# Issuing the second row gather of each pair beside the first, and normalizing three ticks earlier in even steps

## The chip, the cores and the metric

The kernel runs on one core of one Trainium2 chip. The metric is the device time of one launch in microseconds (us), given as the median of several runs. A profile of one execution gives a span, from the first to the last instruction of the program, and what each engine did in it: TensorE (PE), VectorE (DVE), ScalarE (ACT), GpSimd (POOL) and the queue that issues plain DMAs (SP).

## What is computed

A batch of 16 graphs with 1024 nodes and 128 features goes through two layers, each with a residual.

```python
h = relu(layernorm(x)); x = x + attention(h, adj)      # layer 0: softmax over neighbours
h = relu(layernorm(x)); x = x + sage3(h, adj, nodemask) # layer 1
# sage3 starts with this, on each graph's 1024x1024 adjacency:
def step(carry, n):                 # n = 0..1023, each row depends on the rows before it
    row = carry[n]; num = row.sum()
    sf = (num + 1) // 2 if num > 10 else 1
    rm = row & (cumsum(row) % sf == 0) & (num > 1)
    carry[n] = row & ~rm; carry[:, n] &= ~rm
# then three rounds of (adj_d @ h) / deg, two matmuls with weights, l2 norm, relu, batch norm,
# and one last matmul on the three results side by side
```

The sequential pass over rows is called dilation here. A row with 2 to 10 neighbours left at its turn loses them all, so the kernel finds by a bound the rows that may have more (at most 128 per graph), gathers only those rows of the adjacency from memory, and solves the rule for them by a fixed number of iterations.

## The kernel before

**Stages.** The first stage runs 16 steps, one per graph. A step computes scores and values of attention for its graph, and beside them, in pieces, the preparation of later work. From 770 us on a second stage does the first round of layer 1 (function `mix`), together with the rest of the dilation of the last four graphs. Two more rounds and the output follow.

**Ticks.** A step has 48 ticks. Its body is a loop over 16 score tiles (`scores`, L704: two hardware matmuls each); a tick follows the score matmul, and each of the two groups of value matmuls (`values`, L720) that come after it. So there is one score tile in three ticks, and its number times three is the tick. At every tick a hand-written agenda advances generators: each generator is a function cut by `yield` into parts, and a list gives the tick of each part. Parts are emitted in the order of the agenda within a tick, and each engine executes what is emitted for it in this order. What reads a result of another engine is often put off by one or more ticks (`later`).

**Beside attention, in step i:** `bound` of graph i (L237 to L244: a few very small matmuls, L240 and L241, then a comparison into `d_away`, L243, eight times in turn), `mirrors` (transposes L193 and their comparison L199), `project` of graph i+1 (normalization, then projections), loading the adjacency of graph i+1 (ACT, L167 and L184), `norms_of_x2` and `store` of graph i-1, and the solver `solve` for groups of four graphs, which is active in steps 5 to 7 and 9 to 15. `project` on POOL has a chain of small operations (`moments`, L583 to L589) and eight normalizations (`normalize`, L595); PE transposes their results (L605). `norms_of_x2` has the same chain of small operations. `store` issues eight indirect DMAs (L547) on POOL.

**Pairs and gathers.** In every odd step the nodes of two graphs are sorted together (`sort`), and then `gather` is planned for both, in 13 parts: four parts build one-hot tiles on DVE (L298, two instructions each); a fifth multiplies them on PE to node numbers (L303); a sixth turns these into row numbers on DVE (L306) and issues the indirect DMA on POOL (L308) that brings up to 128 rows, 512 KB, into the tile `rows`; the seventh scans the rows on DVE (L312), the eighth makes `codes` of them (L315); the ninth transposes these on PE (L319) into a PSUM tile; two parts copy this on ACT (L323); the twelfth multiplies with the one-hots (L327); the thirteenth stores the codes that the solver needs (L330 to L334). `AT_GATHER` (L750) has the ticks of both, counted from the odd step's start: from 48 on they lie in the next, even step. The tiles `rows`, `left`, `codes` and `turned` have one buffer each.

**PSUM.** The results of `bound`, `mirrors`, `sort` and `gather` go to tiles called `pd`, which take turns in two buffers, in the order in which they are emitted. A new tile in a buffer waits until the readers of the tile before in that buffer are done.

**The last pair.** After step 15 the agenda runs 22 ticks more. What then remains of the last gather is advanced evenly over the 120 turns of the second stage (`last_of_dilation`, L915), with empty turns after some parts (`GATHER_IDLE`), and the solver for the last four graphs follows.

Of the kernel before, what the change touches and what calls it, by code (L numbers as in the profile page):

```python
# [9 lines left out]
H16 = mybir.dt.float16  # L10
# [5 lines left out]
P = 128  # L16
B, N, D = 16, 1024, 128
NB = N // P
# [13 lines left out]
S = 2 * P  # L32
# [48 lines left out]
class Dilation:  # L81
# [209 lines left out]
    def gather(self, b):  # L291


        nc = self.nc
        used = self.used[:, b:b + 1]
        onehot = self.pool.tile([P, NB, S], H16, name="onehot", bufs=1)
        for k in range(NB):
            nc.vector.tensor_scalar(onehot[:, k, :], self.iota, self.pick[b - b % 2][:, b % 2, k:k + 1], None, op0=OP.is_equal)  # L298
            if k % 2:
                yield  # L300
        pi = self.bank([P, 1], F32)
        for k in range(NB):
            nc.tensor.matmul(pi, onehot[:, k, :P], self.node16[:, k:k + 1], start=(k == 0), stop=(k == NB - 1))  # L303
        yield
        row = self.pool.tile([P, 1], I32, name="row")
        nc.vector.tensor_scalar(row, pi, float(b * N), None, op0=OP.add)  # L306
        rows = self.pool.tile([P, N], F32, name="rows", bufs=1)
        nc.gpsimd.indirect_dma_start(out=rows, out_offset=None, in_=self.adj.rearrange("b n m -> (b n) m"),  # L308
                                     in_offset=bass.IndirectOffsetOnAxis(ap=row[:, 0:1], axis=0))
        yield  # L310
        left = self.pool.tile([P, N], H16, name="left", bufs=1)
        nc.vector.tensor_tensor_scan(left[:, ::-1], rows[:, ::-1], rows[:, ::-1], 0.0, op0=OP.add, op1=OP.bypass)  # L312
        yield
        codes = self.pool.tile([P, N], H16, name="codes", bufs=1)
        nc.vector.scalar_tensor_tensor(codes, rows, 1023.0, left, op0=OP.mult, op1=OP.add)  # L315
        yield
        pt = self.bank([P, NB, P], H16)
        for k in range(NB):
            nc.tensor.transpose(pt[:, k, :], codes[:, k * P:(k + 1) * P], self.identh)  # L319
        yield  # L320
        turned = self.pool.tile([P, NB, P], H16, name="turned", bufs=1)
        for h in range(2):
            nc.scalar.activation(turned[:, 4 * h:4 * h + 4, :], pt[:, 4 * h:4 * h + 4, :], AF.Copy)  # L323
            yield
        pq = self.bank([P, S], F32)
        for k in range(NB):
            nc.tensor.matmul(pq, turned[:, k, :], onehot[:, k, :], start=(k == 0), stop=(k == NB - 1))  # L327
        yield
        dg = self.pool.tile([P, P], BF, name="dg")
        nc.vector.scalar_tensor_tensor(dg, pq[:, :P], used, self.identf, op0=OP.mult, op1=OP.mult,  # L330
                                       accum_out=self.dcode[:, b:b + 1])
        nc.vector.tensor_scalar(self.own[:, b, :], dg, 512.0, None, op0=OP.is_gt)
        nc.vector.scalar_tensor_tensor(self.code[:, b, :P], pq[:, :P], used, self.up, op0=OP.mult, op1=OP.mult)
        nc.scalar.activation(self.code[:, b, P:], pq[:, P:], AF.Copy, scale=used)  # L334
        yield
# [172 lines left out]
@with_exitstack  # L508
def gnn_kernel(ctx: ExitStack, tc: tile.TileContext, a, out):
    nc = tc.nc  # L510
    with tc.tile_pool(name="verdict", bufs=1) as vp:
        flag = fast(tc, a, out, vp)
        bad = nc.values_load(flag[0:1, 0:1])
    tc.strict_bb_all_engine_barrier()
    with tc.If(bad > 0):
        general(tc, a, out)
# [3 lines left out]
def fast(ctx: ExitStack, tc: tile.TileContext, a, out, vp):  # L520
# [127 lines left out]
    with ExitStack() as s1:  # L648
# [83 lines left out]
        def store(b):  # L732
            for k in range(NB):
# [7 lines left out]
        every = lambda first, n, by: [first + by * j for j in range(n)]  # L741

        AT_PROJECT = [m + every(m[4] + 4, 4, 1) + every(m[4] + 12, 10, 3)
                      for m in ([1, 9, 14, 15, 16], [0, 1, 3, 5, 6])]
        AT_LOAD = every(1, 2 * NB, 3)
        AT_BOUND = [[0] + [first + 3 * (j // 2) + j % 2 for j in range(2 * NB)] for first in (9, 3)]
        AT_MIRRORS = ([11, 20, 23, 29, 33, 35, 39, 42, 44], [11, 13, 16, 19, 22, 25, 29, 33, 41])

        AT_SORT = [27, 29, 31, 32, 33, 35, 36]
        AT_GATHER = ([37, 38, 39, 41, 44, 45, 51, 55, 59, 60, 61, 65, 66],  # L750
                     [68, 69, 70, 71, 74, 75, 81, 85, 89, 90, 91, 93, 94])
        AT_NORMS = ([30, 57, 67, 68, 71], [42, 44, 58, 67, 70])
        AT_STORE = every(75, NB, 2)

# [4 lines left out]
        def plan(gen, start, ticks):  # L759
            agenda.append((gen, [start + t for t in ticks]))  # L760

        def solve_pieces(b0, b1):
            return 9 * ITER + 3 + 13 * (b1 - b0)

        def plan_step(i):
# [13 lines left out]
            if odd:  # L779
                plan(dil.sort(i - 1), start, AT_SORT)  # L780
                for b, ticks in zip((i - 1, i), AT_GATHER):
                    gathering[b] = dil.gather(b)
# [127 lines left out]
    load_x2(2)  # L910


    GATHER_IDLE = {5: 6, 7: 5}

    def last_of_dilation():  # L915

        for part in range(13 - gather_left, 13):
            next(gathering[B - 1])
            for _ in range(1 + GATHER_IDLE.get(part, 0)):
                yield  # L920
# [161 lines left out]
    with tc.tile_pool(name="ps1", bufs=2, space=PSUM, reuse_waits="tile") as ps:  # L1082
# [5 lines left out]

        tick, TICKS1, PIECES1 = 0, 8 * (B - 1), gather_left + sum(GATHER_IDLE.values()) + solve_pieces(LAST, B)
        entering = iter(())  # L1090
# [786 lines left out]
```

## Time and profile before

| | us |
|---|---|
| time, median of 3 runs | 1275.23 (1273.57 to 1277.38) |
| span of the profiled execution | 1230.9 |
| time of the profiled execution as a whole | not given beside the profile |
| PE busy | 1106.3 |
| DVE busy | 883.8 |
| ACT busy | 728.2 |
| POOL busy | 567.2 |

A line of groups has the line, engine, operation, result and inputs with their shapes and the number of instructions; then the busy time, the mean of one in ns, and after the second bar the idle time of the engine just before them with what ended most of it. A line of the timeline has the start in us from the span's start, the length, the engine, the line, the operation, the number of instructions merged, and in brackets the idle time before. The end of a matmul is modelled, so a busy PE is not PE at its peak; starts are measured. A line of busy time by windows has the window, its length, then the busy time and number of instructions of PE, PE's weight loads, DVE, ACT and POOL, then PE's granted clock, the share of the DMA engines and GB/s.

### The profile page before, as it was taken

Reading aid. Unit: us, or ns where it says so; the run is one execution under the profiler, and the core shown is the slowest. Engines: PE = TensorE matmul, PEld = TensorE weight load, DVE = VectorE, ACT = ScalarE, POOL = GpSimd, SP = SyncE. Lnnn points to the kernel's source line nnn. Section 1 sums busy time; section 2 is a strip of 40 time slices with the busy share of each in tenths; the row PEclk is TensorE's granted clock in tenths of the full one; section 3 lists DMA queues with packets and bytes.
Section 4 is the critical chain, followed back from the end, with each engine's and each line's share of the span. In section 5 each row is a group of like instructions: output and inputs, shape, how many; then the busy total and the mean of one; then the engine's idle time right before and its main releaser. Section 6 shows DMA issues by size and latency. Waiting matters only on the chain.

```text
span 1230.9 us, 22315 instructions
## 1 busy us (share of the span) xinstructions
PE 1106.3 (90%) x7787; PEld 824.2 (67%) x7787; DVE 883.8 (72%) x2630; ACT 728.2 (59%) x1570; POOL 567.2 (46%) x1043
## 2 busy tenths in 40 slices
PE   7899999999899899899889888778769979999896
PEld 3566676666576576567567656667657868888775
DVE  6767567579778678778777868688887876666632
ACT  5578788677678678678677752346554543333221
POOL 0330752651743643644535434687410003777775
PEclk8899999999899999999999999889999999999998
DMA  6544244344234344344333410334000012877664
GB/s 209 148 135 138 87 140 153 106 124 150 87 120 152 103 125 155 95 129 139 109 114 106 130 59 27 96 101 115 1 1 1 1 32 78 237 232 214 195 184 134
DMA packets 118146, 143.44 MB, mean 117 GB/s; under 512 B 9212, under 2 KB 94088, under 8 KB 118024
## 3 DMA queue, kind: packets, MB, share of 16 engines
q1 hardware_dynamic: 106120, 110.78, 30.1%
q0 software_dynamic: 11904, 31.15, 7.7%
q8 instruction: 63, 1.03, 0.4%
q14 instruction: 59, 0.48, 0.1%
HBM read 113.39 MB, written 28.51 MB: 115 GB/s over the span
## 4 chain that ended last, share of the span: by engine, by line
PE 56%; DVE 23%; ACT 6%; POOL 6%; issue 4%; DMA 4%; POOLq 0%; DVEq 0%; ACTq 0%; SPq 0%
PE ps L704 10%; PE po L720 10%; PE po L970 6%; PE pm L683 6%; DVE e L707 4%; DMA rows<-in_adj_dram,row 4%; PE pt L1026 3%; PE ph L1194 2%; PE ph L1251 2%; DVE left L312 2%; PE ph L1195 2%; POOL hn L595 2%; PE po L975 2%; ACT e L706 2%; DVE m L369 2%
## 5 line engine op out<-in xcount | busy, mean ns | idle before, releaser
L720 PEld LDWEIGHTS po<-vw,e 128*128 128x128 f32 x2048 | 274.0, 195 | 66.5 <-issue 66.1
L720 PE MATMUL po<-vw,e 128*128 128x129 f32 x2048 | 307.8, 285 | 0.0
L704 PE MATMUL ps<-qT,kT 128*128 128x512 f32 x512 | 273.3, 617 | 0.8 <-ACT e L706 0.8
L707 DVE TENSOR_TENSOR e<-e,ab 128x512 f32<-128x512 f32 x256 | 177.6, 695 | 113.0 <-ACT e L706 111.3
L706 ACT ACTIVATE e<-ps 128x512 f32<-128x512 f32 x256 | 153.0, 598 | 108.2 <-PE ps L704 85.4
L547 POOL DMA_INDIRECT x_d<-xt,slot x128 | 143.6, 1122 | 39.8 <-issue 36.1
L167 ACT ACTIVATE ab<-st,d_one_k 128x1024 bf16<-128x1024 f32 x128 | 146.8, 1147 | 0.0
L583 POOL TENSOR_SCALAR ln_t<-ln_st 128x8 f32<-128x8 f32 x31 | 8.0, 260 | 290.3 <-DVE ln_st L576 233.2
L184 ACT ACTIVATE junk<-st 128x1024 bf16<-128x1024 f32 x112 | 118.2, 1056 | 0.0
L547 POOL DMA_INDIRECT y_d<-y,nodes x88 | 86.5, 983 | 28.9 <-issue 28.3
L729 ACT ACTIVATE o<-po,recips 128x128 f32<-128x128 f32 x128 | 46.8, 368 | 72.4 <-DVE recips L727 72.2
L704 PEld LDWEIGHTS ps<-qT,kT 128*128 128x128 f32 x512 | 79.1, 194 | 8.2 <-issue 3.7
L595 POOL TENSOR_SCALAR hn<-xt,ln 128x128 f32<-128x128 f32 x120 | 76.4, 648 | 1.6
L1038 ACT ACTIVATE r<-pt 128x512 f32<-128x512 f32 x74 | 44.4, 601 | 55.3 <-PE pt L1026 55.3
L984 ACT ACTIVATE sq<-po 128x512 f32<-128x512 f32 x80 | 47.7, 596 | 48.0 <-PE po L975 44.0
L970 PE MATMUL po<-ws,r 128*128 128x128 f32 x512 | 72.8, 286 | 0.0
L1035 DVE BATCH_NORM_STATS2 stats<-r 128x6 f32<-128x512 f32 x74 | 50.8, 687 | 29.2 <-ACT r L1038 29.2
L987 DVE TENSOR_REDUCE nrm<-sq 128x4 f32<-128x512 f32 x80 | 53.9, 676 | 24.6 <-ACT sq L984 23.3
L312 DVE TENSOR_TENSOR_SCAN left<-rows 128x1024 f16<-128x1024 f32 x16 | 38.9, 2432 | 45.1 <-DMA rows<-in_adj_dram,row 45.1
L1169 POOL COPY mark<-y 128x1 f32<-128x1 f32 x30 | 5.8, 192 | 137.1 <-DVE y L1043 134.5
L970 PEld LDWEIGHTS po<-ws,r 128*128 128x128 f32 x512 | 63.0, 194 | 8.6 <-issue 6.8
L199 DVE SCALAR_TENSOR_TENSOR junkv<-pd,ab 128x64 bf16<-128x64 int32 (+7 forms) x128 | 57.8, 451 | 15.1 <-PE pd L193 15.1
(303 smaller groups left out, 2433.2 us busy)
## 6 DMA issues: line engine op xcount, KB each, us to landing
st<-in_adj_dram SPq DMA_DIRECT2D x128, 512.0 KB, 3.7
r<-y_d SPq DMA_DIRECT2D x22, 512.0 KB, 6.5
xt<-x_d SPq DMA_DIRECT2D x16, 524.0 KB, 4.0
xt<-in_x_dram SPq DMA_DIRECT2D x16, 512.0 KB, 4.3
x<-x_d SPq DMA_DIRECT2D x16, 512.0 KB, 4.6
out_dram<-r SPq DMA_DIRECT2D x11, 512.0 KB, 3.3
x_d<-xt,slot POOLq DMA_INDIRECT x128, 2.8
y_d<-y,nodes POOLq DMA_INDIRECT x88, 5.4
```

Source lines behind the costliest of these rows:

```text
L167: nc.scalar.activation(ab[:, k, :], st, AF.Exp, bias=self.one_k, scale=ONE_K, accum_out=self.deg[:, b, k:k + 1])
L184: nc.scalar.activation(junk(), st, AF.Exp, scale=-ZERO_K, accum_out=zeros)
L199: nc.vector.scalar_tensor_tensor(junk.rearrange("p a b -> p (a b)")[:, :n], pt.rearrange("p a b -> p (a b)").bitcast(I32)[:, :n], 1.0, ab[ ...
L312: nc.vector.tensor_tensor_scan(left[:, ::-1], rows[:, ::-1], rows[:, ::-1], 0.0, op0=OP.add, op1=OP.bypass)
L547: d = nc.gpsimd.indirect_dma_start(out=dst, out_offset=bass.IndirectOffsetOnAxis(ap=slots, axis=0), in_=src, in_offset=None)
L595: engine.tensor_scalar(hn[:, k, :], xt[:, k, :D], minus[:, k // 2, k % 2, None], rstd[:, k // 2, k % 2, None], op0=OP.add, op1=OP.mult)
L683: nc.tensor.matmul(pp, w, hT[:, 512 * g:512 * g + 512], start=True, stop=True)
L704: nc.tensor.matmul(p, K[b][:, k * P:(k + 1) * P], Q[b][:, c], start=True, stop=True)
L706: later(1, lambda: nc.scalar.activation(e, p, AF.Exp))
L707: later(2, lambda: nc.vector.tensor_mul(e, e, AB_[b][:, k, c]))
L720: nc.tensor.matmul(po[:, q % 2, :], E[k][:, i * P:(i + 1) * P], V[b][:, k, :], start=(k == 0), stop=(k == NB - 1))
L970: nc.tensor.matmul(po[:, i, :], hT[:, c:c + P], wxk, start=(i == 3), stop=False)
```

## The change

Four edits. The second gather of each pair has its first six parts (one-hots, node numbers, row numbers and DMA) at ticks 48 to 61 instead of 68 to 75; its scan stays at tick 81 and all later parts where they were. The first gather of each pair has these six parts at ticks 37 to 41 instead of 37 to 45; its scan stays at 51. The one-hot tile gets a second buffer, since the second gather's one-hots are now written before the first gather has read its own for the last time (tick 65). In even steps the normalization for the next graph is planned 2 to 3 ticks earlier, and with it all later parts of `project` by 3 ticks. And since the last gather's DMA is now issued within the 22 extra ticks, the six empty turns after its sixth part are taken out.

```diff
-        onehot = self.pool.tile([P, NB, S], H16, name="onehot", bufs=1)
+        onehot = self.pool.tile([P, NB, S], H16, name="onehot", bufs=2)
...
         AT_PROJECT = [m + every(m[4] + 4, 4, 1) + every(m[4] + 12, 10, 3)
-                      for m in ([1, 9, 14, 15, 16], [0, 1, 3, 5, 6])]
+                      for m in ([1, 7, 11, 12, 13], [0, 1, 3, 5, 6])]
...
-        AT_GATHER = ([37, 38, 39, 41, 44, 45, 51, 55, 59, 60, 61, 65, 66],
-                     [68, 69, 70, 71, 74, 75, 81, 85, 89, 90, 91, 93, 94])
+        AT_GATHER = ([37, 37, 38, 39, 40, 41, 51, 55, 59, 60, 61, 65, 66],
+                     [48, 50, 54, 57, 60, 61, 81, 85, 89, 90, 91, 93, 94])
...
-    GATHER_IDLE = {5: 6, 7: 5}
+    GATHER_IDLE = {7: 5}
```

## The prediction

> **What bounds the kernel now.** I read the page first, then the list of waits, then the timeline of each engine around two places of step 4, the busy time by windows, and the spacing of the score matmuls (L704, one per three ticks). The page's chain of work is more than half PE and a quarter DVE; its 4% of DMA is nearly all the gathered rows. The groups and the list of waits name the stall: the scan L312 kept DVE idle 45.1 us, nine times, 7.4 at the longest.
> ```profile
> PE 56%; DVE 23%; ACT 6%; POOL 6%; issue 4%; DMA 4%; POOLq 0%; DVEq 0%; ACTq 0%; SPq 0%
> ...
> L312 DVE TENSOR_TENSOR_SCAN left<-rows 128x1024 f16<-128x1024 f32 x16 | 38.9, 2432 | 45.1 <-DMA rows<-in_adj_dram,row 45.1
> ```
> ```profile
> DVE left L312 <- DMA rows<-in_adj_dram,row: 45.1, 9, 7.4
> ```
> The timeline (start, length, engine, line, count, idle before) shows why: all eight second gathers wait, the first ones hardly (0.73 us once).
> ```profile
> 221.40 0.15 DVE L306 TENSOR_SCALAR row<-pd 128x1 int32<-128x1 f32 x1
> ...
> 225.26 2.27 POOL L595 TENSOR_SCALAR hn<-xt,ln 128x128 f32<-128x128 f32 x4
> ...
> 227.69 1.07 POOL L308 DMA_INDIRECT rows<-in_adj_dram,row  x1 [0.15 <-issue]
> ...
> 232.36 2.29 DVE L312 TENSOR_TENSOR_SCAN left<-rows 128x1024 f16<-128x1024 f32 x1 [6.39 <-DMA rows<-in_adj_dram,row]
> ```
> The row numbers are ready at 221.55, POOL takes them at 227.69 behind eight normalizations and two chains of small operations, 4.7 us later the rows land. Meanwhile PE waits for the normalized blocks and then for what the stalled DVE owes ACT; the two L704 matmuls here took 1.91 us where two take 1.02 elsewhere, at half clock:
> ```profile
> 226.28 1.63 PE L605 MATMUL pm<-identf,hn 128*128 128x128 f32 x4 [1.00 <-POOL hn L595]
> ...
> 228.39 1.91 PE L704 MATMUL ps<-qT,kT 128*128 128x512 f32 x2
> ...
> 238.58 1.13 PE L683 MATMUL pm<-hT,w_L_gnn_Wk 128*128 128x512 f32 x2 [1.02 <-ACT qT L684]
> ```
> The first gather's place in the same step shows the other limit: DVE has no free time there (window: length, then busy PE, PEld, DVE, ACT, POOL).
> ```profile
> 205.00:212.00 7.00, 6.66 (x45) 4.62 (x44) 7.00 (x12) 5.92 (x14) 0.00 (x0) 1.00 0.43 147
> ```
> ```profile
> 209.11 0.62 PE L319 MATMUL pd<-d_id,codes 128*128 128x128 f16 x8 [0.34 <-DVE codes L315]
> ...
> 210.48 0.17 PE L240 MATMUL pd<-d_away,ab 128*128 128x2 bf16 x1
> ```
> ```profile
> 211.23 0.60 ACT L323 ACTIVATE turned<-pd 128x512 f16<-128x512 f16 x1
> ...
> 211.96 0.62 ACT L323 ACTIVATE turned<-pd 128x512 f16<-128x512 f16 x1
> ```
> Step lengths, from the first L704 of each step to the next: even steps 2 to 14 take 45.8, 46.1, 53.5, 46.7, 49.5, 52.4, 53.2 us, odd ones 3 to 13 take 43.6 to 46.3. For each PE instruction I took the time to the next one less what its kind usually takes. In ticks 30 to 41 of the seven even steps this excess is 5.3, 5.6, 7.5, 5.3, 6.3, 7.7, 7.3 us, together 45.0; in odd steps about 0.3 each. That is what there is to win in the attention stage.
>
> **What the Trainium skill says.** "Perfetto Trace Analysis", Tensor Engine Instruction: ACT, DVE and GPSIMD are strict FIFO. The trace agrees: nothing runs on DVE from 225.97 to 232.36. "DMA: Bandwidth & Descriptors", Anatomy of one DMA (SWDGE): a fit of 2.0 us plus bytes over 436e3; for these 524,288 bytes an estimate of 3.2 us. The trace has 4.7 from issue to landing, which I use. "TensorE: Matmul & The Clock Gate", Part 1: the array falls to half rate after an idle window of about 3.4 us. Here the clock record has half-speed stretches of 3.4 or 6.8 us, at 139, 228, 330, 515, 620 and 716 us in the attention steps, after windows with only some 1.3 to 3.2 us idle; L704 then takes 1061 instead of 592 ns. Nothing is said of the PSUM wait that decides my loss.
>
> **The change part by part**, against the profiled span of 1230.9 us. The profile gives no whole time of its own execution; 1275.23 less 1230.9 leaves 44.3 around the span, which I hold fixed.
>
> 1. Second gather issued at tick 61 instead of 75. In the built order it stands on POOL ahead of the even step's small operations (L583 on), where POOL idles 12.8 us (to 213.35). It costs the same 1.07 us, pushing these operations by that much. It lands about 6 us later, some 12 ticks before the scan at tick 81: the eight waits, 44.3 us of DVE idling, go.
>
> 2. Normalization of even steps 3 ticks earlier (rstd at 13, blocks at 17 to 20): all eight blocks now precede the second chain of small operations (4.7 us), so the transposes at 25 and 28 should find them ready. Together 1 and 2 take the 45.0 us of excess down to the usual 0.3 per step. I leave 0.3 more in the three light steps, 0.5 in step 10 and 1.2 in steps 6, 12, 14, where the solver shares DVE with scan and codes (2.29 + 1.22 us) between ticks 33 and 41: 45.0 - 7 x 0.3 - 5.0 = **38 us won**.
>
> 3. The second gather's one-hots move to ticks 48, 50, 54, 57, into the window where DVE is full. A pair costs 0.39 us (two at 216.99, next instruction 217.38). Three pairs stand ahead of the first gather's codes, four ahead of the reciprocal (L727): codes 1.2, reciprocal 1.6 us later, and PE's transposes L319 wait 1.2 us longer. Afterwards DVE has 1.6 us less to do.
>
> 4. A new wait. The index matmuls (L303) at tick 60 now take a "pd" buffer between the transposes L319 (tick 59) and the next matmul of the bound (L240, tick 60). There are two buffers, so L240 takes the buffer of L319 and must wait for both copies L323; the built program has this wait in all seven even steps. Before, it started at 210.48, with the other buffer. The second copy ends at 212.58; it stands behind o (L729), which waits for the reciprocal, so it ends 1.6 later, at 214.2. PE is 3.7 us later at this point (1.2 of it from item 3), and all value and score matmuls queue behind L240. The same difference in the other steps is 3.7, and 3.0 in step 8, whose 0.73 us wait goes: 6 x 3.7 + 3.0 = 25.2 us lost. Later waits for d_away and the like in ticks 15 to 26 (beyond the usual 0.2 per slot: 1.4 us in steps 6 and 14, 1.9 in 12, 0.8 in 10) vanish when PE comes later: I give back these 5.5. Cheapest case: other work was late anyway and nothing is lost; dearest: see the rival below.
>
> 5. Half clock. Two pauses of 1.8 and 2.4 us within 6 us can bring such a stretch; it costs 1.7 us (half of 3.4). I take it in half the steps: 3.5 x 1.7 = 6 us lost, from 0 to 7 x 3.4 = 24.
>
> 6. First gather of a pair issued at 41, not 45: its one-hots end at 194.8 in step 3, the index matmul comes up at 195.1, no wait; in step 7 about 0.5, in step 15 about 1: **1.5 lost**. A second one-hot buffer only removes a wait for L327 of tick 65.
>
> 7. The end. 13 parts of the last gather less 6 that are done remain, and six empty turns go. The DMA is issued at about 791 instead of 797.2 (behind four stores on POOL, 1.3 us each), lands near 796 instead of 802.5. DVE bounds this stretch; I take the 3.3 us of its wait less what the one-hots delay: **3 won**, from 0 to 6.
>
> Sum: 38 - 25.2 + 5.5 - 6 - 1.5 + 3 = 13.8 us. Span 1217, time 1275.2 - 13.8 = 1261.4.
>
> **Rivals.** *The new PE wait is covered* (items 4 and 5 nearly free, because PE's lateness there is only repaid later by a lighter DVE): 38 + 3 - 1.5 less about 5 for item 3 is 35, so 1240. For it: PE pauses at the same place already (0.5 to 2 us). Against: L240 did start 2.1 us before the second copy's end. *The wait is dear, slower than before*: the pauses at ticks 57 to 60 bring a double half-speed stretch (6.8 us, cost 3.4, as at 330) in each even step. Wins are 38 + 3 + 5.5 - 1.5 = 45, so it turns at 6.4 us lost per even step; 3.6 + 3.4 = 7.0 gives 49, and with DVE's backlog growing by another 0.3 a step 1281. *It only moves the stall*: single stretches everywhere and waits of 1 us left in ticks 30 to 41 bring 6 + 5 back: about 1274. That the DMA isn't earlier is excluded by the order on POOL and the idle time there.
>
> **Chances.** The forecast's own case (1254 to 1270) 50%, wait covered (1232 to 1254) 20%, only moved (1270 to 1279) 15%, dear (above 1279) 15%. About 0.3%, 3.8 us, is what a measurement can tell from no change, so faster 0.68, same 0.17, slower 0.15. The range leaves out the lower third of the covered case and the upper part of the dear one.
>
> **What would show it.** L312 without DMA waits; L308's issue right after row; L605 no longer waiting for hn; ticks 30 to 41 of even steps short by about 5 us; L240 waiting for ACT turned L323, 2 to 2.5 us, seven times, and L319 waiting 1.2 us longer. Wrong if L240 does not wait, if half-speed stretches are more than seven, or if the waits for codes reach the second gather.

## The result, and the profile after

The changed kernel took 1281.84 us (median of 20 runs, 1270.4 to 1292.57) beside 1274.48 for the kernel before on the same chip: ratio 1.0043, 95% interval 1.0026 to 1.0061. The ratio is taken without runs in a slower state (one of these 20, 1292.57, was in it), so it is not the quotient of the two medians. The forecast was 1261.4 us. Measured twice more, the ratio was 1.0052 (1.0018 to 1.0086) and 1.0001 (0.9984 to 1.0018). One thing must be known to read the numbers. The kernel before takes about 1229 us on some chips and about 1275 on others, so only ratios, and profiles from one chip or from chips of one kind, are compared below. The profile of before that the prediction used (span 1230.9) is of the 1229 kind, while its 1275.23 and the profile of after shown first are of the other. Each chip was measured at one time only, so it may also be a condition of that time; "kind" means no more than which of the two times the kernel before takes. In every later run the time of the profiled execution exceeds its span by about 1.8 us; the 44.3 us that the prediction held fixed "around the span" was the difference of two chips.

The page of after, its chain of work: DMA, 4% before and nearly all of it the rows, is down to 1%.
```profile
PE 61%; DVE 22%; ACT 6%; POOL 3%; issue 3%; another core or an unknown queue 1%; DMA 1%; DVEq 0%; SPq 0%; POOLq 0%; ACTq 0%
```
The list of waits of after (engine, tile and line, what it waited for: us in all, times, longest):
```profile
PE pd L319 <- DVE codes L315: 19.3, 8, 5.7
PE pd L240 <- ACT turned L323: 12.9, 7, 1.9
...
PEld pm L605 <- POOL hn L595: 9.4, 18, 2.0
...
DVE left L312 <- DMA rows<-in_adj_dram,row: 7.9, 1, 7.9
```
Eight of nine waits for rows are gone; the one left is the last graph's, in the second stage. In their place stands the forecast wait of L240, seven times. The timeline of step 4 of after (start, length, engine, line; idle before in brackets):
```profile
214.77 0.62 PE L319 MATMUL pd<-d_id,codes 128*128 128x128 f16 x8 [1.32 <-DVE codes L315]
...
216.48 0.34 PE L303 MATMUL pd<-d_node,onehot 128*128 128x1 f16 x8 [0.18 <-DVE d_away L243]
...
218.01 0.62 ACT L323 ACTIVATE turned<-pd 128x512 f16<-128x512 f16 x1
...
218.68 0.16 PE L240 MATMUL pd<-d_away,ab 128*128 128x2 bf16 x1 [1.86 <-ACT turned L323]
...
218.81 0.16 DVE L306 TENSOR_SCALAR row<-pd 128x1 int32<-128x1 f32 x1
...
219.24 1.07 POOL L308 DMA_INDIRECT rows<-in_adj_dram,row  x1 [17.56 <-DVE ln L579]
...
225.33 4.78 POOL L595 TENSOR_SCALAR hn<-xt,ln 128x128 f32<-128x128 f32 x8
...
228.24 0.60 PE L605 MATMUL pm<-identf,hn 128*128 128x128 f32 x4
...
229.13 1.02 PE L704 MATMUL ps<-qT,kT 128*128 128x512 f32 x2
...
234.19 2.28 DVE L312 TENSOR_TENSOR_SCAN left<-rows 128x1024 f16<-128x1024 f32 x1
...
239.23 1.02 PE L683 MATMUL pm<-hT,w_L_gnn_Wk 128*128 128x512 f32 x2
```
The DMA goes out 0.27 us after the row numbers (218.97 to 219.24; 6.1 us before), the scan starts 15 us later without idle time, L605 and L683 do not wait at this place, and L704 is at full clock here. The price: L319 waits 1.32 us instead of 0.34, and L240 stands 1.86 us until the second copy, begun at 218.01, is done. DVE is still full there (window: length, then busy PE, PEld, DVE, ACT, POOL):
```profile
208.00:215.00 7.00, 5.68 (x36) 3.96 (x35) 7.00 (x16) 6.09 (x12) 0.00 (x0) 1.00 0.33 130
```
So most of the forecast signs are there, and yet the time is not shorter. One of the signs of being wrong is there too: the clock record of this profile has eight half-speed stretches after step 0, where more than seven were named.

### The profile page after: what moved, and what is told of

The parts are those of the page before. It is cut to its first block, busy times and chain, and to the rows that moved or that the text cites. A ratio compares the mean times of both kernels' runs of the same rounds, so it can differ in the third digit from the quotient of the medians.

```text
span 1281.6 us, 22306 instructions
## 1 busy us (share of the span) xinstructions
PE 1129.2 (88%) x7787; PEld 841.2 (66%) x7787; DVE 880.2 (69%) x2630; ACT 729.6 (57%) x1570; POOL 569.7 (44%) x1043
## 3 DMA queue, kind: packets, MB, share of 16 engines
q1 hardware_dynamic: 106120, 110.78, 29.3%
## 4 chain that ended last, share of the span: by engine, by line
PE 61%; DVE 22%; ACT 6%; POOL 3%; issue 3%; another core or an unknown queue 1%; DMA 1%; DVEq 0%; SPq 0%; POOLq 0%; ACTq 0%
PE po L720 12%; PE ps L704 11%; PE po L970 6%; PE pm L683 6%; PE pt L1026 3%; DVE e L707 3%; PE ph L1251 3%; PE ph L1194 2%; PE pd L193 2%; PE ph L1195 2%; ACT e L706 2%; PE po L975 2%; DVE m L369 2%; DVE left L312 2%; DVE stats L1035 2%
## 5 line engine op out<-in xcount | busy, mean ns | idle before, releaser
L720 PEld LDWEIGHTS po<-vw,e 128*128 128x128 f32 x2048 | 278.0, 197 | 66.9 <-issue 66.5
L720 PE MATMUL po<-vw,e 128*128 128x129 f32 x2048 | 313.7, 288 | 0.0
L704 PE MATMUL ps<-qT,kT 128*128 128x512 f32 x512 | 276.8, 625 | 0.8 <-ACT e L706 0.8
L706 ACT ACTIVATE e<-ps 128x512 f32<-128x512 f32 x256 | 152.7, 597 | 150.6 <-PE ps L704 92.8
L547 POOL DMA_INDIRECT x_d<-xt,slot x128 | 141.0, 1101 | 39.5 <-issue 33.1
L308 POOL DMA_INDIRECT rows<-in_adj_dram,row x16 | 16.6, 1039 | 211.0 <-DVE ln L579 116.0
L547 POOL DMA_INDIRECT y_d<-y,nodes x88 | 86.5, 983 | 29.2 <-issue 29.2
L704 PEld LDWEIGHTS ps<-qT,kT 128*128 128x128 f32 x512 | 80.8, 198 | 7.4 <-issue 2.9
L1035 DVE BATCH_NORM_STATS2 stats<-r 128x6 f32<-128x512 f32 x74 | 51.0, 689 | 35.8 <-ACT r L1038 30.8
L595 POOL TENSOR_SCALAR hn<-xt,ln 128x128 f32<-128x128 f32 x120 | 71.8, 612 | 1.6
```

The source lines that it names most:

```text
L547: d = nc.gpsimd.indirect_dma_start(out=dst, out_offset=bass.IndirectOffsetOnAxis(ap=slots, axis=0), in_=src, in_offset=None)
L595: engine.tensor_scalar(hn[:, k, :], xt[:, k, :D], minus[:, k // 2, k % 2, None], rstd[:, k // 2, k % 2, None], op0=OP.add, op1=OP.mult)
L704: nc.tensor.matmul(p, K[b][:, k * P:(k + 1) * P], Q[b][:, c], start=True, stop=True)
L706: later(1, lambda: nc.scalar.activation(e, p, AF.Exp))
L720: nc.tensor.matmul(po[:, q % 2, :], E[k][:, i * P:(i + 1) * P], V[b][:, k, :], start=(k == 0), stop=(k == NB - 1))
L1035: nc.vector.bn_stats(stats[:, 2 * b + g, :], d)
```

## Where the time went, on one chip

Runs e9 (before) and e10 (after) are from one chip of the 1229 kind: medians 1227.91 and 1229.01, profiled executions 1225.84 and 1231.1, spans 1224.0 and 1229.3. As in the prediction, I took for each PE instruction the time to the next one less what its kind usually takes, and summed by ticks. In the table even steps are 2 to 14 and odd ones 3 to 13; where the length of the odd steps together is given further down (314 us for the kernel before), step 1 is in it.

| us | before, e9 | after, e10 | won (+) | forecast |
|---|---|---|---|---|
| even steps, ticks 30 to 41 | 42.3 | 3.0 | +39.3 | +38 |
| even steps, ticks 9 to 17 | 16.2 | 47.0 | -30.8 | -25.2 - 6 |
| even steps, ticks 18 to 29 | 9.6 | 5.4 | +4.2 | +5.5 |
| odd steps, ticks 18 to 29 | 4.4 | 9.4 | -5.0 | 0 |
| odd steps, other ticks | 13.3 | 15.0 | -1.7 | in the -1.5 below |
| start to the end of step 0, and step 1 | | | -2.0 | 0 |
| step 15 | 8.1 | 11.3 | -3.2 | -1.5 |
| last score matmul to L1242 (end of second stage) | 384.5 | 391.1 | -6.6 | +3 |
| last stage | 73.0 | 73.4 | -0.4 | 0 |

The rows sum to 6.2 lost; the spans differ by 5.3. The even steps win 12.7 net of 12.3 forecast. What was lost is outside them. By length the even steps go from 343.8 to 337.1 us and the odd ones from 314.1 to 315.5: the earlier plan has moved one projection per pair of steps from the odd step into the even one, and the table leaves out what an instruction usually takes. These are single profiles. The even steps of the kernel before take 340.3 us in e1, 343.8 in e9 and 347.1 in the profile that the prediction used, and the start to the end of step 0 takes 67.4 to 70.3 us over all profiles; so rows of some 2 us tell nothing, and larger ones are read below together with other runs. The waits of e9 and then of e10:
```profile
DVE left L312 <- DMA rows<-in_adj_dram,row: 44.8, 9, 7.3
...
PE pd L319 <- DVE codes L315: 11.2, 8, 4.3
...
PE pm L605 <- POOL hn L595: 9.2, 8, 2.3
```
```profile
PE pd L319 <- DVE codes L315: 19.0, 8, 5.4
PE pd L240 <- ACT turned L323: 12.6, 7, 1.9
...
DVE left L312 <- DMA rows<-in_adj_dram,row: 7.2, 1, 7.2
```

## The experiments

**One part alone, on a chip of the 1229 kind.** e1 is the kernel before itself.

> The kernel before, unchanged, profiled a second time. The two profiles at hand differ by 50.7 us in span (1230.9 and 1281.6) while the medians differ by 7.4 us, and 23 us of that lie in the last stage, which the change doesn't touch. Theory A (the first profile of before is a quick execution, and what it lacks is no effect of the change): a span near 1272, with the last stage (from the first copy L1242 to the end) near 83 us instead of 59, and waits of ACT in odd steps too. Theory B (the change slows the odd steps and the last stage): a span near 1231 again, last stage 59 us, odd steps 43.5 to 46.5 us. Ratio to before 1.000 in both.

Measured 0.9992 (0.9971 to 1.0013), span 1220.6. The 1230.9 of the old profile is a usual span on such a chip. Theory B was right on the span; the last stage takes 73 us in both profiles of the kernel before, not the 59 expected.

e2 has the earlier normalization alone:
```diff
-                      for m in ([1, 9, 14, 15, 16], [0, 1, 3, 5, 6])]
+                      for m in ([1, 7, 11, 12, 13], [0, 1, 3, 5, 6])]
```


> Only the normalization of even steps is planned earlier; both gathers stay as before. Theory A (PE's wait for normalized blocks at ticks 28 to 31 costs some 2 us in five even steps, and nothing else comes in): 8 to 12 us faster, about 1264; the scan still waits for its rows some 6 us in each even step. Rival (the gather's DMA and its wait set the end of these ticks, the blocks only wait beside it): within 3 us of before.

Measured 1.0030 (1.0012 to 1.0048). My theory fell: it wins nothing, and the rival was right in kind.

e3 has the earlier second gather alone:
```diff
-        onehot = self.pool.tile([P, NB, S], H16, name="onehot", bufs=1)
+        onehot = self.pool.tile([P, NB, S], H16, name="onehot", bufs=2)
...
-                     [68, 69, 70, 71, 74, 75, 81, 85, 89, 90, 91, 93, 94])
+                     [48, 50, 54, 57, 60, 61, 81, 85, 89, 90, 91, 93, 94])
...
-    GATHER_IDLE = {5: 6, 7: 5}
+    GATHER_IDLE = {7: 5}
```


> Only the second gather is moved (ticks 48 to 61, second one-hot buffer, no empty turns); the first gather and the normalization stay as before. Theory A (the second gather's move wins some 4 us a step in ticks 33 to 41 and loses 3.7 in ticks 57 to 60; the earlier normalization is what wins the rest): about 1276 to 1282, the same as before or slower than the whole change by some us. Rival (what makes the change slow is the earlier normalization or the earlier first gather): faster than the whole change, 1265 to 1272.

Measured 0.9954 (0.9934 to 0.9974). In its even steps the excess in ticks 30 to 41 is 6.5 us, so the gather alone removes nearly all of the 42 us; in ticks 9 to 17 it is 48.8. In e11, the same kernel again, about 11 us are left in ticks 30 to 41. The rival was right: alone, the earlier gather is faster than the whole change.

e4 is the changed kernel with the index matmuls of the second gather after the bound's tick:
```diff
-                     [48, 50, 54, 57, 60, 61, 81, 85, 89, 90, 91, 93, 94])
+                     [48, 50, 54, 57, 64, 65, 81, 85, 89, 90, 91, 93, 94])
```


> The whole change, but the second gather's index matmul and DMA at ticks 64 and 65 instead of 60 and 61, so that the bound's matmul at tick 60 finds a free PSUM buffer. Theory A (the wait of L240 for the copies L323, 2.3 us in each of seven even steps, is what turns the gain into a loss): that wait is gone and the time falls by 10 to 16 us against the whole change, to 1266 to 1272. Rival (PE's pause is shared with DVE's backlog, which the one-hots make, and with stalls in odd steps): falls by 5 us at the most, 1277 to 1282.

Measured 0.9970 (0.9956 to 0.9984). Ticks 9 to 17 of its even steps cost 34.4 us instead of e10's 47.0, but odd steps cost more: 8.0 in ticks 0 to 8 and 12.1 in ticks 18 to 29. The ratio is 0.3% under e10's on the same kind of chip: the rival's "5 us at the most", not the theory's 10 to 16.

**The changed kernel and three between, on a chip of the 1275 kind.** e5 is the changed kernel.

> The changed kernel as it is, on the chip of the runs beside it. Theory (the four parts add up: the earlier second gather wins 5 to 8 us, its index matmuls at tick 60 cost about 5 us, the earlier normalization costs about 4, the idle turns taken out of the end cost about 6): ratio 1.002 to 1.006, and by profile odd steps 5 to 10 us longer in sum than those of the kernel before, and some 6 us more from the last score matmul to the first normalization of the following stage (L1066). Rival (the long odd steps of the first profile of this kernel, 342.9 us against 314.2, and its last stage of 96 us against 73, belong to the chip of that comparison): the ratio comes out at 0.999 or less here, odd steps within 325 us, last stage at 73.

Measured 1.0052 (1.0018 to 1.0086). The long odd steps (337.2 us against 314) and the long last stage (97.7) are there again. They are in every kernel on this chip, so the rival was right on what they belong to and wrong on the ratio.

e6 is e3 with the old line `GATHER_IDLE = {5: 6, 7: 5}`, e7 is e6 with the index matmuls at 64 and 65 as in e4, e8 is the changed kernel with the old normalization line (the reverse of e2's edit).

> Second gather early, everything else as in the kernel before, and unlike e3 the six idle turns ahead of the last gather's DMA wait are kept. Theory (the turns let other work fill DVE while the last rows land; without them the stretch from the last score matmul to L1066 was 157.3 us in e3 against 151.2 in e1): that stretch is back at about 151, and the time 5 to 6 us under e3's ratio 0.9954, so 0.990 to 0.992. Rival (DVE's total work bounds that stretch, and the 6 us come from elsewhere): as e3, 0.994 to 0.997, and the stretch stays at 156 to 158.

> As e6, and the index matmuls of the second gather at tick 64 instead of 60, so that L240 at tick 60 has its old PSUM buffer back. Theory (the wait of L240 for both copies costs even steps 1 to 3 us each): even steps together 7 to 15 us shorter than in e6, ratio 0.980 to 0.986. Rival (that wait only takes the place of later waits for d_away): within 3 us of e6.

> The changed kernel with the normalization of even steps back at its old ticks; first gather early, second gather early, idle turns taken out. Theory (the earlier normalization has no wait of its own to remove once the scan no longer waits, and its transposes then wait for POOL in odd steps): 4 to 6 us faster than e5, odd steps together back near 314 us. Rival (the first gather's earlier ticks are what lengthens the odd steps): within 1.5 us of e5, odd steps as long as there.

Measured 0.9998 (0.9970 to 1.0026), 1.0061 (1.0041 to 1.0080) and 1.0042 (1.0019 to 1.0066). e7 missed on the wrong side: its even steps take 357.1 us, e6's 341.2. e8's odd steps stay long (336.2), as all do on this chip, and its ratio cannot be told from e5's. In e6 the stretch to L1066 came back to about 151 us as expected, but the ratio lies outside both of its ranges.

**The pair, and two repeats, the 1229 kind.** e9 and e10 are the pair above; e11 repeats e3, e12 repeats e2.

> The kernel before, unchanged, for its profile beside those of the next three on one chip (the chips of the comparisons so far stand at 1229 and at 1275 us for it). Theory (the slower chip stalls ACT and PE while POOL issues its rows of indirect stores, L547, in every version): ratio 0.998 to 1.002; on a chip near 1275 the odd steps take 335 to 340 us in sum instead of 314, with L683 waiting for ACT kT L684, and the last stage about 93 instead of 73. Rival (those stalls come from the change): odd steps near 314 on such a chip too. On a chip near 1229 it repeats e1.

> The changed kernel. On a chip near 1229 us, theory (gather wins 6, norm loses 5, index matmuls at 60 instead of 64 lose 5 against e4's 0.997): 0.999 to 1.003; rival (the index matmuls' tick is worth nothing): as e4, 0.996 to 0.998. On a chip near 1275, as in the two comparisons there: 1.003 to 1.007.

> As e3, the earlier second gather alone, without the six idle turns. On a chip near 1229: again 0.993 to 0.997. On a chip near 1275, theory (idle turns are worth 6 us there too): 5 to 6 us over e6's 0.9998, so 1.004 to 1.005; rival (they are worth nothing): 0.998 to 1.001.

> As e2, the earlier normalization alone. Theory (it removes no wait: the 45 us in ticks 30 to 41 hang on the scan's wait, and come back as waits of L193 and L683 behind it): 1.002 to 1.005 on either chip. Rival (on a chip near 1275 it hides some of the stalls at the stores): under 1.000 there.

Measured 0.9998 (0.9983 to 1.0013), 1.0001 (0.9984 to 1.0018), 0.9954 (0.9936 to 0.9972), 1.0051 (1.0031 to 1.0072), all as expected for a chip of this kind. The waits of e12 show why the earlier normalization alone wins nothing:
```profile
DVE left L312 <- DMA rows<-in_adj_dram,row: 37.0, 9, 6.0
...
PE pm L683 <- ACT kT L684: 8.5, 5, 1.9
...
PE pd L193 <- DVE junkv L199: 6.4, 5, 2.0
```
DVE still stands 37 us for the rows; PE passes L605 sooner and then waits for what DVE and ACT owe it. The 42 us hung on the scan. And odd steps lose: 9.4 us in ticks 18 to 29, as in e10, where e3, e9, e11 and e13, with the old normalization, have 4.3 to 4.4. The edit moves the projections with the normalization, one of them from an odd step into the even one; PE then reaches the odd step's transposes L605 sooner than POOL has normalized: in odd steps it waits 2.8 us for the blocks in e10 and e12, and not at all in e9.

**The idle turns, the index matmuls, the stores, the 1229 kind.** e13 is e6 again. e14 is the changed kernel with the old `GATHER_IDLE` line. e15 is e13 with the index matmuls at 62 and 63. e16 is the kernel before with one edit:
```diff
-        AT_STORE = every(75, NB, 2)
+        AT_STORE = every(81, NB, 2)
```


> As e6: second gather early, idle turns kept, the rest as before. On a chip near 1229 us, theory (idle turns are worth 6 us): 0.989 to 0.992, and 384 to 386 us from the last score matmul to the first copy of the last stage (L1242) as in the kernel before, instead of 391. Rival (they are worth nothing, something else in the end is longer): as e3 and e11, 0.994 to 0.997, and 390 to 392. On a chip near 1275: again 0.997 to 1.003.

> The changed kernel with the six idle turns back. Theory: 5 to 6 us under the changed kernel: 0.995 to 0.996 on a chip near 1229, 1.000 on one near 1275; 385 us from the last score matmul to L1242. Rival: as the changed kernel, 1.000 and 1.005.

> As e13 with the index matmuls of the second gather at tick 62 and 63, behind the bound's L240 of ticks 60 and 61. Theory (that L240 waits for both copies of turned costs 2 to 3 us of each even step in e3): even steps together 8 to 14 us shorter than in e13, time 7 to 12 us less. Rival (the pause comes anyway a few ticks later, as DVE is full there): within 3 us of e13.

> The kernel before with its stores in the attention stage (L547) six ticks later. Theory (on the slower chip ACT and PE stall while POOL issues these stores): on a chip near 1275 the waits for ACT kT L684 and the idle ACT of odd steps move from ticks 33 to 39 to ticks 39 to 45, and their sum stays within 10 us. Rival (the stalls belong to those ticks' own work, the K projections): they stay at ticks 33 to 39. On a chip near 1229 there are none in either place, and the time stays within 0.3%.

Measured: e13 0.9942 (0.9923 to 0.9961), e14 0.9961 (0.9947 to 0.9975), e15 1.0054 (1.0034 to 1.0074), e16 1.0274 (1.0246 to 1.0303).

*The idle turns.* From the last score matmul to L1242 e14 takes 385.9 us and e13 385.8, e10 391.1 and e11 390.0. So the old line is worth about 5 us there by profile; by medians 4.2 (e14 1224.86, e10 1229.01; the ratios' intervals do not overlap), and 3 to 4 for e13 beside e3 and e11, where the ratios' intervals overlap. e13's stretch is the one expected, while its ratio lies in the rival's range. Over all profiles on chips of the 1229 kind the stretch is 390 to 392 us without the old line (four profiles) and 384 to 388 with it. But the turns do not help for my reason: DVE waits 7.2 us for the last rows in e14 as in e10. In these kernels six parts of the last gather are done when the second stage begins, so the turns after part 5 are never taken with either line: they only count in `PIECES1`, the number that sets the pace at which the rest (parts and solver) is advanced over 120 turns. With them it is 7 + 11 + 118 = 136 (13 parts less 6; 9 x 7 + 3 + 13 x 4 = 118 solver pieces), without them 130, and 130 pieces exist. The kernel before has four more parts left and takes the turns: pace 140, 140 pieces. The pace decides how much solver work DVE has beside the mixes. Here are the busy times (window: length, then busy PE, PEld, DVE, ACT, POOL, then the granted clock) of e9 and e10 in the 60 us that begin 40 us after the last score matmul:
```profile
807.00:867.00 60.00, 51.61 (x426) 43.41 (x425) 54.31 (x146) 38.14 (x142) 47.48 (x101) 0.99 0.31 82
...
805.20:865.20 60.00, 51.22 (x391) 44.33 (x389) 49.33 (x129) 34.85 (x128) 45.35 (x94) 0.89 0.34 92
```
DVE is busy 54.3 us before and 49.3 after, and 54.6 in e14; it waits 0.6, 9.0 and 1.7 us there for what ACT gives to L1035. In all seven profiles without the old line DVE is busy 48.9 to 49.8 us of these 60, in the other thirteen 52.7 to 55.2. The solver work that is missing there comes later: the last L451 comes 138.0 us after the last score matmul in e9, 144.0 in e10 and 133.8 in e14. What the lower clock of e10 (0.89) adds was not separated. Before graph 15's `mix` the code drains the rest, and L1066 of the next round comes at 152.6 us in e14 and 158.2 in e10.

*A wait that keeps two others away.* e15 takes the wait of L240 away and is 1.1% slower than e13; both of its expectations missed. Its waits, and then e13's:
```profile
PE pm L605 <- POOL hn L595: 19.3, 7, 3.7
```
```profile
PE pd L240 <- DVE row L306: 9.5, 6, 1.8
```
In e15 ticks 9 to 17 cost 34.5 us (e13 48.8), but ticks 30 to 41 cost 36.1 (6.5): PE stands before L605 until POOL has normalized, up to 3.7 us at once, with half clock after it. As its line shows, L240 waits in six of the seven steps of e13 (in e3, e6 and e11 too) for the row numbers of L306, and once for the copies; in e10, e14 and e18 it waits for the copies seven times. Why the buffers fall differently was not looked into. Counted from the start of steps 2, 4 and 8, PE comes to the first transposes 2.4 us sooner in e15 than in e13 (22.8 instead of 25.2 in step 2), and POOL's last block is ready 2.9 us later (30.1 instead of 27.2). The timeline of step 4 of e15 shows where most of the 2.9 arises:
```profile
230.88 2.28 DVE L312 TENSOR_TENSOR_SCAN left<-rows 128x1024 f16<-128x1024 f32 x1
...
230.95 3.77 POOL L595 TENSOR_SCALAR hn<-xt,ln 128x128 f32<-128x128 f32 x4
...
233.47 1.77 PE L605 MATMUL pm<-identf,hn 128*128 128x128 f32 x4 [3.20 <-POOL hn L595]
```
The four blocks take 3.77 us, 2.16 in e13: the first of them, begun 0.07 us after the scan on DVE, takes 2.47 instead of 0.45 and ends 0.26 us after the scan. In step 4 of e13 the scan comes later, when POOL is at its stores. So PE's pause at L240 held PE back and also kept the scan behind the normalization; the two shares are read from the trace and were not tried apart.

*Stores later.* e16 met no chip of the 1275 kind, so it does not test what it was made for; that its time would stay within 0.3% elsewhere was wrong by far (2.7%). It shows another thing, in its waits:
```profile
ACT ab L167 <- DMA st<-in_adj_dram: 37.4, 6, 8.4
...
PE ps L704 <- ACT e L706: 28.1, 6, 6.6
```
Later stores (L547, POOL) free a buffer of x later; SP waits with the load of the next x (L658: 211.0 us in all, 153.0 in e9), the adjacency loads (L166) are queued behind it, and ACT waits for them in the even steps.

**Both waits gone, the 1229 kind.** e17 is e15 with the normalization earlier and its transposes and projections at their old ticks; e18 is the same with the index matmuls at 60 and 61.
```diff
-        AT_PROJECT = [m + every(m[4] + 4, 4, 1) + every(m[4] + 12, 10, 3)
-                      for m in ([1, 9, 14, 15, 16], [0, 1, 3, 5, 6])]
+        AT_PROJECT = [m + every(m[4] + 4, 4, 1) + every(first, 10, 3)
+                      for m, first in (([1, 7, 11, 12, 13], 28), ([0, 1, 3, 5, 6], 18))]
```


> Second gather early, idle turns kept, index matmuls at tick 62, normalization (DVE and POOL part) of even steps 3 ticks earlier with transposes and projections at the old ticks. Theory (PE's lateness in an even step is the larger of the two waits, not their sum): with both gone, even steps together 322 to 330 us against e13's 336, odd steps 314; time 7 to 13 us under e13, ratio 0.984 to 0.989. Rival (a third wait takes their place, DVE being full to tick 20): within 3 us of e13's 0.9942.

> As e17 with the index matmuls at tick 60, ahead of L240, so that its wait for the PSUM buffer is back. Theory: the pause behind that wait already gave the normalization its time, so the earlier normalization is worth nothing here: as e13, 0.993 to 0.995, and 6 to 12 us over e17, which is the price of the wait of L240. Rival (the price of that wait is 1 us or less once the normalization is early): within 2 us of e17.

Measured 1.0017 (1.0005 to 1.0029) and 0.9948 (0.9932 to 0.9964). In e17 the even steps take 322.6 us, as expected (e18 333.4, e13 335.8), so by these single profiles the wait of L240, without its cover, is worth 10.8 us (the same step from e10 to e4 takes 11.0 off them); but the odd steps take 338.8 (e18 317.6, e13 314.0). A third wait took their place, as the rival said, at a higher price than it said (e17 is 0.8% slower than e13); e18's ratio is the one expected, but it is the faster of the two and not the slower. The waits of e17:
```profile
ACT ab L167 <- DMA st<-in_adj_dram: 16.7, 5, 4.2
PE pm L691 <- ACT hn L684: 15.9, 5, 4.0
```
The timeline of e17 where step 5 begins (at 247.5), and of e18 (at 245.8), shows its way:
```profile
245.61 0.97 POOL L547 DMA_INDIRECT x_d<-xt,slot  x1 [0.30 <-issue]
...
248.21 0.38 SPq L658 DMA_DIRECT2D xt<-in_x_dram  x1
...
248.69 1.47 SPq L166 DMA_DIRECT2D st<-in_adj_dram  x3
...
254.42 1.15 ACT L167 ACTIVATE ab<-st,d_one_k 128x1024 bf16<-128x1024 f32 x1 [4.17 <-DMA st<-in_adj_dram]
```
```profile
240.11 0.96 POOL L547 DMA_INDIRECT x_d<-xt,slot  x1 [0.30 <-issue]
...
242.77 0.38 SPq L658 DMA_DIRECT2D xt<-in_x_dram  x1
```
The last store is done 42.4 us after the start of step 4 in e17 (246.58 less 204.2) and 41.1 after it in e18 (241.07 less 200.0). Over all even steps of these two kernels the last store is done 40.7 to 45.3 us after the step's start. A step that PE finishes in 43.3 us (e17) so leaves SP no time to load ahead, one of 45.8 (e18) does.

e13 has the lowest ratio of all, 0.9942 (0.9923 to 0.9961) beside the kernel before and 0.6% under that of the changed kernel on like chips (1.0001), but on a chip of the 1275 kind the same kernel (e6) is level with the one before.

## Why the prediction was wrong

On the first chip the kernel became slower, against the forecast's sign; on the other kind of chip about nothing was won, where 13.8 us were forecast. The steps can be compared on that other kind alone, where both kernels have a profile. By its steps:

**1, the earlier second gather: right for seven of the eight.** The waits in the attention stage are gone, and the DMA is issued 0.27 us after the row numbers. The eighth second gather is the last graph's; it still waits, see step 7.

**2, 38 won in ticks 30 to 41: right in size (39.3), wrong in cause and in price.** The gather alone does it (e3: 6.5 us left), the normalization alone does not (e12: 33.7 left). And the shift was costed at nothing elsewhere: it costs odd steps 5.0 us in ticks 18 to 29 (e10, e12), 2.8 of them PE's wait for POOL's blocks. This is gone where the projections stay at their old ticks (e18 has 4.1 us in these ticks, about as the kernel before) or the normalization does (e3, e13). As an edit alone it is 0.3 to 0.5% slower.

**3 and 4, one-hots and the wait of L240: right in kind, the sum about right.** L319 waits for codes 7.8 us more than before and L240 12.6, in seven waits of up to 1.9; ticks 9 to 17 lose 30.8, forecast 31.2 with the half clock. What I did not see is what the pause keeps away: without it the scan falls on POOL's normalization and PE waits at L605 (e15), and without both, the loads behind POOL's stores come too late (e17).

**5, half clock: about right in size.** By the clock record, e9 has five half-speed stretches after step 0 in the attention stage, 17.1 us in all, and e10 seven, 30.7 us. Half of the 13.6 us more is an estimate of 6.8 lost, for 6 forecast; it lies within the rows of the table. On the 1275 kind the profile of after has eight, 51.2 us in all, but there is no profile of the kernel before to set beside it.

**6, the first gather: too small.** Step 15 loses 3.2 us for 1 forecast. By length, step 15 takes 42.5 to 43.9 us in all profiles with the early first gather (after, e4, e5, e8, e10, e14) and 39.9 to 40.6 in those without it, but for e7 with 42.9.

**7, the end: this step failed, in sign.** I forecast 3 won from the earlier rows, and 6.6 were lost. The 3.3 us of DVE's wait for the last rows did not go but became 7.2: counted from the last score matmul the DMA is issued 23.5 us after it instead of 27.3, and the scan, which no longer has other parts and turns ahead of it in the second stage, is reached 7.7 us earlier (21.6 instead of 29.3). Nor does DVE bound the stretch: I took the six empty turns as turns that go, and did not read that they also set the pace of the solver, so that DVE has too little work for a while and too much of it at the end; e14 gives 4 to 5 of the 6.6 back with that line alone, though its DVE waits the same 7.2. This step is 9.6 of the 20.0 us by which the table misses its forecast.

Steps 2, 6 and 7 are what turned the sum: 12.7 won in even steps, 18.9 lost outside them. Of the rivals none was right. The first chip's 1281.84 us lie in the range of the dear pause, by luck as far as the profiles tell: even steps, where it puts the loss, were not where the sum failed. "It only moves the stall" has the right sum for the 1229 kind, no change, but not its cause, since 3.0 us are left in ticks 30 to 41; its 6 + 5 also give 1272 and not 1274. The base was wrong as well, since 44.3 us around a span do not exist.

**Open.** On chips of the 1275 kind the two kernels that met both kinds stand some 0.5% worse against the one before than on the others (e6 0.9998, e13 0.9942, the same program; the changed kernel 1.0043 and 1.0052, e10 1.0001). No profile of the kernel before was taken there, so where it is spared these 6 us is not settled. It may be that even steps of before hide part of that chip's delays in their wait for rows; this is only argued.

## What to carry to other kernels

Before paying for a removed wait, list the other waits that end shortly after it (here PSUM buffer, POOL's normalization, a load behind POOL's stores): a pause on PE may be the time in which another queue keeps up, and taking it away alone cost 1% here. Ask also what else runs when a long instruction moves: here the scan on DVE moved onto POOL's normalization. A constant that looks like padding may also stand in a sum that sets a pace: follow each number of an edit to all its uses. Take a span and a time from the same execution before adding them.

## What the runs showed of the hardware

The same program differs by 54 us between chips: e13 took 1220.08 us, e6 1274.16; the spans of their profiles differ by 48.6. By profile, attention step by step, the odd steps take 314.0 and 336.6 us, the even ones 335.8 and 341.2, the last stage 72.8 and 92.8, and the stretch between 385.8 and 386.2. In odd steps the delays lie where POOL issues its stores; ACT's timeline in e6:
```profile
282.68 0.20 ACT L167 ACTIVATION_READ_ACCUMULATOR ab<-st,d_one_k 128x1 f32 x1
285.66 0.60 ACT L706 ACTIVATE e<-ps 128x512 f32<-128x512 f32 x1 [2.78 <-PE ps L704]
```
ACT is idle 2.78 us although PE issued the score matmuls at 280.89 and 281.32 and went on at once; in e3, at the same place on the other kind of chip, L706 follows without a gap. That it falls on the stores was seen, that they cause it was not tried with success (e16 met the other kind of chip).

In the attention stage of e15 every POOL instruction that begins while the scan runs on DVE (2.28 us) ends with the scan or later. A block of L595 takes 2.47 us instead of 0.45 (steps 2, 4 and 8), small operations of L588 and L589 take 2.11 and 2.13 instead of 0.20. In the kernel before the scan falls on stores alone (2.0 to 2.6 us instead of 0.97 in e9). It was the other way round once: the last graph's scan in e9 took 4.58 us while POOL's blocks beside it took 0.44.
